# Local attention's values: two projected spans of 128 tokens a batch instead of three

## Chip, cores and metric

The kernel runs on one core of one Trainium2 chip. The metric is the device time of one execution in microseconds, taken as the median of several runs. All data are float32 except a few bfloat16 copies of weights outside the part that changes.

## What is computed

A two-layer decoder block on `x` (4 batches of 256 tokens, width 256) with a context of 1601 tokens a batch: sliding-window attention, attention over the context, a quantised feed-forward part, a second attention, a linear attention over the context and a mixture of experts, each followed by a residual and a layer norm. The change is in the first part, the sliding-window attention with 16 heads of 16. Cut to what matters:

```python
C = 64                                              # chunk and window
kc = concatenate([kp[:, :, :-1], kp[:, :, 1:]], -2) # keys: the chunk before, and this chunk
vc = concatenate([vp[:, :, :-1], vp[:, :, 1:]], -2)
diff = C + qa[:, None] - ka[None, :]
mask = (diff >= 0) & (diff <= WINDOW)               # and the key's position not negative
scores = where(mask, einsum('bhncd,bhnkd->bhnck', qc, kc) * SCALE, -inf)
out = einsum('bhnck,bhnkd->bhncd', softmax(scores), vc)
```

A query attends to itself and to the 64 tokens before it. The values are `x @ w_v`, one row for each token; softmax and the weighted sum don't depend on the order in which a query's keys stand, as long as scores, mask and values have the same order.

## The kernel before

The whole program is one function, `decoder`. Its helper functions don't issue instructions as they are called: they record operations, and `Loom.weave` (line 309) then plays the program through as a list scheduler. It takes each time the operation that can start earliest by assumed durations (`Side.cost`, line 402, and the figure given to each `piece` of TensorE work), with an order of priorities to break ties, and lets idle engines of one part work on another part. The order on every engine, of the DMA issues too, is thus written out when the program is built; on the chip, each engine runs its own list in order and waits on semaphores. Because one helper issues everything, all lines of the profile on DVE, ACT and POOL read L398, all matmuls L261, all transposes L268 and all ordinary loads L275; a group is told by its tiles.

`l0_attention(b)` (line 673) is recorded for the four batches with the highest priority. After the queries and keys of a batch (`qT`, `kT`, the latter in two copies for the even and odd heads of a pair, each with the other's rows at zero) come the values. Tile `v` (two of them, for even and odd batches) has the shape (128 tokens, 3 spans, 8 head pairs, 2, 32); the half of the last axis that isn't written stays at the zero that POOL put there at the start. Before, three spans of 128 tokens are projected, starting at token 0, 64 and 128 (span `i` starts at 64 x i): two matmuls of 128x256 each (the width of 256 is summed in two halves), and then one copy on DVE for the even heads and one on ACT for the odd ones.

`unit(j)` (line 696) does eight heads. Its first piece, "scores", has four matmuls for queries 0 to 127 against keys 0 to 127 (tiles of 32 rows by 128 columns of the array, one for each pair of heads), and then eight for the other queries: 64 queries 128 to 191 against keys 64 to 191 (`c` = 0), and 64 queries 192 to 255 against keys 128 to 255 (`c` = 1), in tiles of 32 rows by 64 columns. Each of the four score banks then gets the mask `wmask` added on DVE, a softmax (maximum on DVE, four exponentials on ACT, a reciprocal on DVE, a product on DVE or POOL), four transposes into a bank, and an evacuation into `aT`. The last piece, "pv", multiplies with span 0 for the queries 0 to 127, span 1 for 128 to 191 and span 2 for 192 to 255. Two such units make a batch; an output projection, residual and norm follow.

Around it, with a lower priority, `context_sums` (line 764) works on the context for the linear attention of the second layer: pieces "keys" (`KT` by `wkv1`), a feature map on ACT and DVE (`fm`, `kf`), pieces "sums" (`V` by `kf`), and an addition on POOL (`kacc`). Those sums, and products of weights for later layers, fill TensorE while local attention's softmax runs, and continue after it. All score, projection and transpose results go through one pool of eight PSUM banks (`bank`).

The masks are made at the start on POOL: a memset of `wmask` (128 x 2 x 128) and of a helper tile `lower`, two selections (`keep_where`, line 555) for each of three masks, and a copy on DVE of the lower half of the second mask out of `lower`.

Of the kernel before, what the change touches and what calls it, by code (L numbers as in the profile page):

```python
# [31 lines left out]
P = 128  # L32
# [10 lines left out]
NEG = -1e30  # L43
# [138 lines left out]
class Loom:  # L182
# [62 lines left out]
    @contextmanager  # L245
    def piece(self, us, claims=(), ins=(), over=(), what=""):


        self.cur = ([], [], list(ins))
        yield  # L250
        fns, outs, ins = self.cur
        self.cur = None
        read = [o for v in over for _, o in v.buf.reads]
        self.op({"PE": (us, us, lambda: [f() for f in fns])}, outs, ins, claims, after=read, what=what)

    def mm(self, o, lhsT, rhs, start, stop, **kw):
        fns, outs, ins = self.cur
        outs.append(o)
        ins += [v for v in (lhsT, rhs) if isinstance(v, View)]
        fns.append(  # L260
            lambda: self.nc.tensor.matmul(real(o), real(lhsT), real(rhs), start=real(start), stop=stop, **kw)  # L261
        )

    def turn(self, o, x, ident):
        fns, outs, ins = self.cur
        outs.append(o)
        ins += [x, ident]
        fns.append(lambda: self.nc.tensor.transpose(real(o), real(x), real(ident)))  # L268
# [156 lines left out]
def decoder(ctx: ExitStack, tc: tile.TileContext, a: dict, out: bass.AP):  # L425
    nc = tc.nc
    k = Loom(tc)
# [39 lines left out]
    def bank(shape=(P, 512), dtype=F32, acc=False):  # L467
        return psB.tile(shape, dtype, "bank", free=True, acc=acc)
# [20 lines left out]
    def evac(dst, src):  # L489

        return either((k.vector, "tensor_copy", (dst, src), {}), (k.scalar, "copy", (dst, src), {}))
# [63 lines left out]
    def keep_where(t, pattern, base, cm, fill):  # L555
        k.gpsimd.affine_select(
            out=t, in_=t, pattern=pattern, compare_op=ALU.is_ge, fill=fill, base=base, channel_multiplier=cm
        )
# [3 lines left out]

    wmask = p1w.tile((P, 2, P), F32, "wmask")
    lower = p1.tile((P, 2, 2, P), F32, "at", bufs=7)[:, 0, 0]
    k.gpsimd.memset(wmask, 0.0)
    k.gpsimd.memset(lower, 0.0)
    for m, off in ((wmask[:, 0], 0), (wmask[:, 1], 64), (lower, 0)):
        keep_where(m, [[-1, P]], off, 1, NEG)
        keep_where(m, [[1, P]], 64 - off, -1, NEG)
    k.vector.tensor_copy(wmask[64:, 1], lower[64:])  # L570

    hmask = const.tile((P, 8, 17), F32, "hmask")
# [15 lines left out]
    for i in range(2):  # L588
        v = p1w.tile((P, 3, H // 2, 2, 32), F32, f"v{i}")
# [10 lines left out]
    def new_x():  # L600
        return xpool.tile((P, 2, D), F32, "x")
# [29 lines left out]
    def norm(b, x):  # L631
        X[b], XT[b] = x, new_xt()
        norm_into(x, XT[b])

    def softmax(at):

        n = at.shape[2]
        nm, ss, rs = (tiny((P, 4), tag) for tag in ("nm", "ss", "rs"))
        k.vector.tensor_reduce(nm, at, AX.X, ALU.max, negate=True)
        for i in range(4):  # L640
            k.scalar.activation(at[:, i], at[:, i], AF.Exp, bias=nm[:, i : i + 1], accum_out=ss[:, i : i + 1])
        k.vector.reciprocal(rs, ss)
        args = (at, at, rs.unsqueeze(2).to_broadcast([P, 4, n]), ALU.mult)
        either((k.gpsimd, "tensor_tensor", args, {}), (k.vector, "tensor_tensor", args, {}))
# [18 lines left out]
    def project_in(xt, w, claims=(), what=""):  # L663

        ps = bank((P, 2, S))
        with piece(1.73, claims, what=what):
            for j in range(2):
                for c in range(2):
                    mm(ps[:, j, :], w(c, j), xt[:, c, :], c == 0, c == 1)
        return ps  # L670


    def l0_attention(b):
        pool = p1


        kT = pool.tile((P, 2, 2, S), F32, "kT")
        ps = project_in(XT[b], lambda c, j: wqkv[:, c, D + j * P : D + (j + 1) * P], [kT], "k")
        k.vector.tensor_scalar(kT[:, :, 0, :], ps, qmask[:, 0:1], None, ALU.mult)
        k.scalar.activation(kT[:, :, 1, :], ps, AF.Copy, scale=qmask[:, 1:2])  # L680
        qT = pool.tile((P, 2, S), F32, "qT")
        ps = project_in(XT[b], lambda c, j: wqkv[:, c, j * P : (j + 1) * P], [qT], "q")
        evac(qT, ps)
        v = vs[b % 2]
        for i in range(3):
            pv = bank((P, D))
            with piece(0.86, over=[v], what="v"):
                for c in range(2):
                    mm(pv, XT[b][:, c, 64 * i : 64 * i + P], wqkv[:, c, 2 * D :], c == 0, c == 1)
            heads = pv.rearrange("p (h u e) -> p h u e", u=2, e=16)  # L690
            k.vector.tensor_copy(v[:, i, :, 0, :16], heads[:, :, 0, :])
            k.scalar.copy(v[:, i, :, 1, 16:], heads[:, :, 1, :])
        xn = new_x()
        oT = pool.tile((P, 2, S), F32, "oT1", bufs=1)

        def unit(j):

            quarters = [slice(32 * r, 32 * r + 32) for r in range(4)]
            pss = [bank((P, 2, 2, P)) for _ in range(4)]
            ats = [pool.tile((P, 2, 2, P), F32, "at", bufs=7) for _ in range(4)]  # L700
            with piece(1.5, ats, what="scores"):
                for rr, ps in zip(quarters, pss):
                    mm(ps[:, 0], qT[rr, j, :P], kT[rr, j, :, :P], True, True, skip_group_check=True)
                for c in range(2):
                    for r, (rr, ps) in enumerate(zip(quarters, pss)):
                        mm(
                            ps[64 * c : 64 * c + 64, 1],
                            qT[rr, j, P + 64 * c : P + 64 * c + 64],
                            kT[rr, j, :, 64 + 64 * c : P + 64 + 64 * c],
                            True, True, skip_group_check=True,  # L710
                            tile_position=(32 * r, 64 * c),
                        )
            aTs = []
            for ps, at in zip(pss, ats):
                k.vector.tensor_tensor(at, ps, wmask.unsqueeze(2).to_broadcast([P, 2, 2, P]), ALU.add)
                at = at.rearrange("p t u k -> p (t u) k")
                softmax(at)
                pt = bank((P, 4, P))
                aT = pool.tile((P, 2, 2, P), F32, "aT", bufs=4)
                with piece(0.44, [aT], what="turn"):  # L720
                    for i in range(4):
                        turn(pt[:, i], at[:, i], ident)
                evac(aT.rearrange("p t u q -> p (t u) q"), pt)
                aTs.append(aT)
            po = bank((P, S))
            with piece(1.5, [oT], what="pv"):
                for i, q0, n in ((0, 0, P), (1, P, 64), (2, P + 64, 64)):
                    t = q0 // P
                    for u in range(2):
                        for r, rr in enumerate(quarters):  # L730
                            mm(
                                po[rr, q0 : q0 + n],
                                v[:, i, 4 * j + r, u, :],
                                aTs[r][:, t, u, q0 - t * P : q0 - t * P + n],
                                u == 0, u == 1, skip_group_check=True,
                                tile_position=(0, 32 * r),
                            )
            evac(oT[:, j], po)

        for j in range(2):  # L740
            unit(j)
        for t in range(2):
            py = bank((P, D))
            with piece(0.86, [xn], what="out"):
                for j in range(2):
                    mm(py, oT[:, j, t * P : (t + 1) * P], w0o[:, j, :], j == 0, j == 1)
            k.vector.tensor_tensor(xn[:, t, :], py, X[b][:, t, :], ALU.add)
        norm(b, xn)
# [719 lines left out]
    for b in range(B):  # L1468
        at_prio(0, b)
        l0_attention(b)  # L1470
# [47 lines left out]
    for b in range(B):  # L1518
        at_prio(7, b)
        for ts, x, xt in l1_attention(b):  # L1520
# [5 lines left out]
            if b == B - 1:  # L1526
                at_prio(8)
                n = EARLY[ts[0]]
# [93 lines left out]
```

## Time and profile before

| | |
|---|---|
| median of 3 runs | 708.22 us (708.21 to 709.07) |
| the profiled execution's own time | 710.24 us |
| its span | 708.5 us |
| TensorE busy | 664.6 us |
| VectorE (DVE) busy | 447.3 us |
| ScalarE (ACT) busy | 297.4 us |
| GpSimd (POOL) busy | 126.4 us |
| DMA | 87.33 MB, mean 123 GB/s |
| granted TensorE clock, mean | 0.982 |

The profile is of one execution. PE stands for matmuls and PEld for the loading of the stationary operand. A float32 matmul shows as two records of matmul and two of weight loading, which are its two passes; a transpose shows as one. Matmul records overlap, so that the distance between their starts tells more than their lengths. Counts (x...) are of records. A line of groups ends with the idle time of the engine just before the instructions and what ended it.

### The profile page before, as it was taken

How to read it: one execution, taken by the hardware profiler on the slowest of the kernel's cores; microseconds unless marked ns; L12 is line 12 of the kernel's file. 1: busy time of each engine (PE TensorE's matmuls, PEld its weight loads, DVE VectorE, ACT ScalarE, POOL GpSimd, SP SyncE). 2: the span in 40 equal slices, each digit the busy share in tenths (PEclk: the TensorE clock that was granted, in tenths of full speed). 3: DMA queues.
4: the chain of work that ended last, by engine and by line, in shares of the span. 5: the costliest groups of instructions: out<-in, count | busy, mean ns of one | idle time of the engine just before them, and what ended most of it. 6: DMA issues, size and time to landing. Idle time of an engine off the chain costs nothing.

```text
span 708.5 us, 12388 instructions
## 1 busy us (share of the span) xinstructions
PE 664.6 (94%) x4407; PEld 531.2 (75%) x4411; DVE 447.3 (63%) x1155; ACT 297.4 (42%) x930; POOL 126.4 (18%) x170
## 2 busy tenths in 40 slices
PE   7999999999999999999899999999998899999970
PEld 5787878568877777767676777767766898999960
DVE  4878896333528634384799978687686555333336
ACT  2868965211132433343358777476455121111100
POOL 3313223012300000000022011221213213111112
PEclk9999999999999999999999999999999999999995
DMA  8922100646998241000010600000002845976405
GB/s 302 351 76 76 52 19 10 205 128 224 331 300 283 67 149 37 1 1 1 0 54 1 237 3 1 1 31 1 30 1 73 318 147 195 364 278 228 147 26 177
DMA packets 62673, 87.33 MB, mean 123 GB/s; under 512 B 4654, under 2 KB 44340, under 8 KB 62612
## 3 DMA queue, kind: packets, MB, share of 16 engines
q1 hardware_dynamic: 60740, 81.40, 35.2%
q0 software_dynamic: 1872, 5.13, 2.0%
q8 instruction: 36, 0.59, 0.3%
q14 instruction: 25, 0.20, 0.1%
HBM read 70.83 MB, written 15.69 MB: 122 GB/s over the span
## 4 chain that ended last, share of the span: by engine, by line
PE 78%; DVE 14%; ACT 3%; DMA 2%; issue 1%; POOL 1%; SPq 0%; POOLq 0%; DVEq 0%
PE bank L261 70%; PE bank L268 8%; DVE at L398 3%; ACT at L398 3%; DVE nm L398 2%; DVE x L398 1%; DVE h L398 1%; POOL rstd L398 1%; DVE as L398 1%; DVE entry L398 1%; DVE st L398 1%; DMA wt<-in_w 1%; DMA back<-yd 1%; DVE kf L398 0%; DVE fm L398 0%
## 5 line engine op out<-in xcount | busy, mean ns | idle before, releaser
L398 ACT ACTIVATE at<-at,nm 128x128 f32<-128x128 f32 (+1 forms) x256 | 106.5, 420 | 25.7 <-DVE nm L398 25.2
L261 PE MATMUL bank<-xgT,wt 128*128 128x128 f32 x736 | 87.0, 278 | 0.8 <-DVE xgT L398 0.5
L261 PEld LDWEIGHTS bank<-xgT,wt 128*128 128x128 f32 x736 | 86.2, 195 | 2.0 <-DVE xgT L398 0.8
L268 PE MATMUL bank<-ident,at 128*128 128x128 f32 (+1 forms) x440 | 61.5, 277 | 1.8 <-DVE at L398 1.6
L268 PEld LDWEIGHTS bank<-ident,at 128*128 128x128 f32 (+1 forms) x440 | 50.8, 142 | 14.3 <-issue 5.9
L261 PE MATMUL bank<-V,aT 128*128 128x256 f32 (+1 forms) x240 | 55.2, 380 | 0.7 <-DVE o L398 0.6
L261 PE MATMUL bank<-KT,qT 128*128 128x512 f32 (+1 forms) x128 | 54.0, 553 | 0.0
L261 PEld LDWEIGHTS bank<-V,aT 128*128 128x128 f32 (+1 forms) x240 | 45.2, 190 | 11.2 <-issue 3.6
L398 POOL TENSOR_SCALAR rstd<-mv 128x2 f32<-128x2 f32 (+1 forms) x26 | 6.5, 251 | 261.6 <-DVE mv L398 215.8
L261 PE MATMUL bank<-kf,V 128*128 128x256 f32 (+1 forms) x208 | 50.4, 383 | 1.1 <-DVE kf L398 1.1
L398 DVE TENSOR_REDUCE nm<-at 128x4 f32<-128x512 f32 (+1 forms) x64 | 50.6, 807 | 0.4
L261 PE MATMUL bank<-wkv,KT 128*128 128x256 f32 (+1 forms) x208 | 49.7, 382 | 0.0
L398 ACT ACTIVATION_READ_ACCUMULATOR at<-at,nm 128x1 f32 x256 | 48.7, 190 | 0.0
L398 ACT ACTIVATE eh<-bank 128x512 f32<-128x512 f32 x23 | 13.7, 597 | 77.5 <-PE bank L261 77.5
L261 PEld LDWEIGHTS bank<-kf,V 128*128 128x128 f32 (+1 forms) x208 | 38.2, 190 | 7.5 <-DVE kf L398 2.3
L398 ACT COPY aT<-bank 128x512 f32<-128x512 f32 (+2 forms) x60 | 31.5, 551 | 29.4 <-PE bank L268 28.6
L261 PE MATMUL bank<-w2e,eh 128*128 x184 | 43.4, 380 | 0.0
L261 PEld LDWEIGHTS bank<-wkv,KT 128*128 128x128 f32 (+1 forms) x208 | 37.8, 186 | 7.3 <-issue 1.5
L398 DVE TENSOR_TENSOR at<-at,rs 128x512 f32<-128x512 f32 (+1 forms) x43 | 39.7, 924 | 0.8
L398 POOL TENSOR_TENSOR at<-at,rs 128x512 f32<-128x512 f32 (+1 forms) x21 | 23.6, 1123 | 87.9 <-DVE rs L398 74.7
L398 ACT ACTIVATE fm<-bank 128x512 f32<-128x512 f32 (+2 forms) x33 | 18.1, 552 | 46.6 <-PE bank L261 46.6
L1258 POOL DMA_INDIRECT yd<-ey,slots x23 | 22.3, 971 | 83.9 <-DVE slots L398 81.9
(246 smaller groups left out, 1231.3 us busy)
## 6 DMA issues: line engine op xcount, KB each, us to landing
wt<-in_w SPq DMA_DIRECT2D x46, 512.0 KB, 4.7
lists<-h SPq DMA_DIRECT2D x6, 1548.0 KB, 16.8
KT<-in_ctxT SPq DMA_DIRECT2D x6, 1024.0 KB, 5.1
V<-in_ctx SPq DMA_DIRECT2D x6, 1024.0 KB, 5.4
w2e<-in_w SPq DMA_DIRECT2D x8, 512.0 KB, 9.1
KT<-in_ctxT SPq DMA_DIRECT2D x6, 577.0 KB, 3.8
V<-in_ctx SPq DMA_DIRECT2D x6, 512.0 KB, 4.0
xg<-lists SPq DMA_DIRECT2D x23, 129.0 KB, 4.3
```

The source lines that it names most:

```text
L261: lambda: self.nc.tensor.matmul(real(o), real(lhsT), real(rhs), start=real(start), stop=stop, **kw)
L268: fns.append(lambda: self.nc.tensor.transpose(real(o), real(x), real(ident)))
L398: return getattr(engine, method)(*[real(x) for x in args], **{k: real(x) for k, x in kw.items()})
L1258: d = nc.gpsimd.indirect_dma_start(out=dst.real(), out_offset=bass.IndirectOffsetOnAxis(ap=row.real(), axis=0), in_=src.real(), in_offset= ...
```

## The change

Only two spans of values are projected in each batch, tokens 0 to 127 and 128 to 255 (`i` = 0 and 2). Span 1 of `v`, which serves the queries 128 to 191 and so needs the tokens 64 to 191, is copied out of the same two banks: partitions 64 to 127 of the first (tokens 64 to 127) stay on partitions 64 to 127, and partitions 0 to 63 of the second (tokens 128 to 191) stay on 0 to 63. Its keys thus stand in another order, 128 to 191 first and 64 to 127 second. The scores for these queries are made in that order: one matmul of 2x128 columns for each pair of heads becomes two of 2x64, with the same stationary operand. Their mask (partitions 0 to 63 of `wmask[:, 1]`) is made anew: forbidden where the key's column is greater than the query's row and less than the row + 64. Each batch has four copies into `v` on DVE and four on ACT, two of each over 128 partitions and two over 64.

```diff
-    k.gpsimd.memset(wmask, 0.0)
+    k.gpsimd.memset(wmask[:, 0], 0.0)
     k.gpsimd.memset(lower, 0.0)
-    for m, off in ((wmask[:, 0], 0), (wmask[:, 1], 64), (lower, 0)):
+    for m, off in ((wmask[:, 0], 0), (lower, 0)):
         keep_where(m, [[-1, P]], off, 1, NEG)
         keep_where(m, [[1, P]], 64 - off, -1, NEG)
+    k.gpsimd.memset(wmask[:64, 1], NEG)
+    keep_where(wmask[:64, 1], [[1, P]], -1, -1, 0.0)
+    keep_where(wmask[:64, 1], [[-1, P]], 63, 1, 0.0)
     k.vector.tensor_copy(wmask[64:, 1], lower[64:])
...
-        for i in range(3):
+
+        for i in (0, 2):
             pv = bank((P, D))
             with piece(0.86, over=[v], what="v"):
                 for c in range(2):
                     mm(pv, XT[b][:, c, 64 * i : 64 * i + P], wqkv[:, c, 2 * D :], c == 0, c == 1)
             heads = pv.rearrange("p (h u e) -> p h u e", u=2, e=16)
-            k.vector.tensor_copy(v[:, i, :, 0, :16], heads[:, :, 0, :])
-            k.scalar.copy(v[:, i, :, 1, 16:], heads[:, :, 1, :])
+            part = slice(0, 64) if i else slice(64, P)
+            for rr, n in ((slice(0, P), i), (part, 1)):
+                k.vector.tensor_copy(v[rr, n, :, 0, :16], heads[rr, :, 0, :])
+                k.scalar.copy(v[rr, n, :, 1, 16:], heads[rr, :, 1, :])
...
-                for c in range(2):
+                for c, to, k0, n in ((0, 0, P, 64), (0, 64, 64, 64), (1, 0, P, P)):
                     for r, (rr, ps) in enumerate(zip(quarters, pss)):
                         mm(
-                            ps[64 * c : 64 * c + 64, 1],
+                            ps[64 * c : 64 * c + 64, 1, :, to : to + n],
                             qT[rr, j, P + 64 * c : P + 64 * c + 64],
-                            kT[rr, j, :, 64 + 64 * c : P + 64 + 64 * c],
+                            kT[rr, j, :, k0 : k0 + n],
                             True, True, skip_group_check=True,
                             tile_position=(32 * r, 64 * c),
                         )
```

## The prediction, made before the changed kernel ran

> **What bounds the kernel now.** I read the page first (busy shares, then the shares of the chain), then busy time by stage, then the chain of waits in order of time inside the stage that the change touches, then the tiles `v`, `wqkv` and `kT`. Page, parts 1 and 4:
>
> ```profile
> span 708.5 us, 12388 instructions
> PE 664.6 (94%) x4407; PEld 531.2 (75%) x4411; DVE 447.3 (63%) x1155; ACT 297.4 (42%) x930; POOL 126.4 (18%) x170
> PE 78%; DVE 14%; ACT 3%; DMA 2%; issue 1%; POOL 1%; SPq 0%; POOLq 0%; DVEq 0%
> ```
>
> TensorE is the bound over all. Whether it is so where the change lies is asked of the stages. Local attention (`l0_attention`) runs from 4 to about 123 us, woven with context sums, which go on with weight products to 197 us; the first scores of cross attention start at 200 us. Busy times by stage:
>
> ```profile
> 4.00:30.00 26.00, 24.52 (x183) 19.36 (x184) 17.11 (x33) 13.56 (x46) 7.64 (x8) 1.00 1.04 364
> 30.00:66.00 36.00, 36.00 (x315) 29.83 (x313) 29.91 (x67) 27.98 (x119) 8.64 (x9) 1.00 0.33 101
> 66.00:111.00 45.00, 44.00 (x481) 35.10 (x478) 42.07 (x95) 36.20 (x152) 10.96 (x12) 1.00 0.14 40
> 111.00:124.00 13.00, 13.00 (x109) 11.03 (x108) 7.65 (x17) 4.64 (x12) 4.94 (x6) 1.00 0.05 14
> ```
>
> The columns are PE, PEld, DVE, ACT, POOL, clock, DMA share and GB/s. From 30 to 66 us PE is never idle and DVE has a sixth free. From 66 to 111 us DVE is busy 42.07 of 45 us, and PE idles 1.0. The chain of waits says the same:
>
> ```profile
> 58.23 6.40 PE bank L261 x72
> 64.63 0.87 PE bank L268 x8
> 65.50 1.38 PE bank L261 x24
> 66.89 0.00 issue
> 66.89 0.68 DVE kf L398
> ...
> 109.73 0.70 DVE at L398
> 110.43 0.04 issue
> 110.48 0.66 PE bank L268 x4
> 111.14 1.73 PE bank L261 x8
> ```
>
> Up to 66.9 us the chain is PE work, then 43.6 us of DVE and ACT steps alone (masks, maxima, exponentials, copies), then PE again. A PE saving ahead of 66.9 us should reach the end; one inside that stretch can be lost as idle PE time, unless context work is moved into it.
>
> **What the skill says.** "Perfetto Trace Analysis", Identifying the Most-Contended Engine, warns that matmul busy time is no measure of PE's limit, since matmuls are pipelined. The trace agrees: one 128x256 record lasts 379 ns, but twelve in a row take 2.75 us, and the next group begins 2.68 us after the first began. So I price matmuls by the distance of starts (0.216 us) and not by duration. "TensorEngine Tiling (Array Packing)", Key Properties, says that tiles work independently and that a change of tiling mode drains the array. The trace agrees with both: eight score matmuls of 32x64 tiles, two records each, take 0.62 us together, and the last full record before the first score takes 0.31 instead of 0.216 us. "TensorE: Matmul & The Clock Gate", The mechanism (Part 3), says that matmuls keep strict program order. Here the trace doesn't quite agree: the second record of a tile's matmul starts 0.267 us after its first, while the other seven tiles' first records start in between, within 0.05 us. I use that rule only for an upper price below.
>
> **What goes away.** Each batch loses one of three value projections: two matmuls, shown as four records. Tiles `wqkv`, `v` and `kT`:
>
> ```profile
> L261 PE MATMUL bank<-wqkv,xt x48: 379/379/483, 10.8 to 77.9; 128*128 128x256 f32 x48
> L398 DVE COPY v<-bank x12: 252/276/292, 11.9 to 82.3; 128x128 f32<-128x128 f32 x12
> L398 ACT COPY v<-bank x12: 239/262/267, 12.2 to 78.3; 128x128 f32<-128x128 f32 x12
> L261 PE MATMUL bank<-kT,qT x192: 374/400/478, 13.5 to 100.8; 32*64 32x256 f32 x128, 32*128 32x256 f32 x64
> ```
>
> 48 records become 32: 16 x 0.216 = 3.46 us of PE time, 0.864 a batch. The projections of batches 0, 1 and 2 start at 10.8, 31.2 and 45.0 us, all before 66.9; those of batch 3 at 70.5 and 77.2, inside the DVE stretch. So 2.59 us of the 3.46 are on the path for sure, and 0.86 only if the weave fills the hole.
>
> **What is added on PE.** For queries 128 to 191 the score matmul of 2x128 keys becomes two of 2x64 with the same stationary operand: 4 more matmuls (8 records) in each of 8 units, columns unchanged. Now, the round lasts 0.62 us: weights 0.053, two passes of 0.213, a drain. The split tile needs 0.053 + 4 x 0.107 = 0.48 us, as long as the unsplit neighbour beside it, weights being loaded under the running pass. If the neighbour (queries 192 to 255, issued last) still starts at once, the price is nothing: tiling covers it. If it starts only when the split tile's second matmul has started, 0.21 us later, the price is 8 x 0.21 = 1.7 us. If it waits for the whole of it, 8 x 0.43 = 3.4 us. The trace of before has no tile with two matmuls queued behind each other and another tile behind them in a 32x64 mode, so these are the bounds; a gain I exclude, since no column goes away. I take 0.85 us, half way between the first two.
>
> **What is added on DVE and ACT.** Each batch has 4 copies into `v` on each, not 3. Two of the four take 64 partitions; by the by-form groups a 65-partition step is no cheaper for that (ACT `fm` 65x256: 362 ns, ACT `oT` copy 128x256: 362). So 4 x 0.275 = 1.1 us DVE and 4 x 0.257 = 1.0 us ACT. Batch 0's fall where DVE had waited 0.57 us for PE between copies: nothing. Those of batches 1 and 2 stand where PE is the bound and DVE has 6 of 36 us free: nothing, as long as that cover lasts. Batch 3's stand on the DVE chain: 0.28, plus up to 0.26 if ACT's is on it too. I take 0.3. Behind these copies on DVE wait the masks and maxima that ACT's exponentials wait for, and on ACT the exponentials that DVE's reciprocals wait for. A projection's bank is freed after four copies instead of two, but two banks are taken instead of three.
>
> **What moves.** The masks on POOL: two memsets (about 0.2 us each, by the 128x128 one's 205 ns) replace one of 0.31, the six selections stay six, all before 4 us; the first mask is used at 14.9 us: nothing, covered by the first load and projections. No DMA is added or removed, and SP's and POOL's queues are passed by no step. But the order on all engines is planned in `weave` from assumed durations, so an 0.86 piece less and two copies more in each batch may order neighbours anew. Known stalls that such a change can remove or repeat:
>
> ```profile
> 14.74 5.45 PE L261 MATMUL bank<-wkv,KT 128*128 128x256 f32 x24
> 21.32 1.99 PE L261 MATMUL bank<-kf,V 128*128 128x256 f32 x8 [1.13 <-DVE kf L398]
> ```
>
> That one is 1.13 us, those of 66 to 111 us sum to 1.0. After 200 us the stages contain far more idle time between small steps (PE idle 8 of 80 us from 480 to 560), so 2 us either way is fair for an order that differs. Nothing there is tied to an absolute time: beyond the first load, PE waits for no DMA before 200 us, and SP's loads wait for PE to free buffers; they come earlier with it.
>
> **The sum.** -2.59 (batches 0 to 2) - 0.43 (half of batch 3's) + 0.85 (scores) + 0.3 (copies) = -1.9 us. The profiled execution had a span of 708.5 and a time of 710.24, so about 1.7 us lie around the span, and it is 2.0 us above the median of the runs, 708.22; the difference is applied to the median: 706.3 us. Its own range, from full filling and free scores (-3.46 + 0.3) to dear scores with batch 3's hole lost (-2.59 + 1.7 + 0.5), is 705.1 to 707.8.
>
> **Rivals.**
> - *The score rounds eat it.* Strict order of matmuls makes the neighbour wait for both halves: 3.4 us against 3.46 saved. About 708.2, no change. For it: in-order issue; against it: eight tiles overlap now.
> - *DVE and ACT become the bound of all of local attention (slower).* Place: 30 to 111 us. DVE is at 93% from 66 us on; if the PE time removed turns into waits on it, the whole saving is lost and three batches' added copies are in series on the chain, 3 x (0.275 + 0.257) = 1.6 us: 709.8. It decides once PE's idle time from 30 to 111 us grows from 1.0 us by the whole saving there, 2.6. Against it: context sums and weight products, 197 - 123 = 74 us more of them, are there to fill PE.
> - *The new order matters more than the work*: some stalls vanish (the 1.13 above, a part of those later), and the time is 2 us under the sum: 704.3; or as much above it.
>
> **Chances.** The sum 0.50, score rounds 0.15, DVE/ACT bound 0.13, a luckier order 0.16, an unlucky one 0.06. What a measurement of this kernel can tell from no change is about 0.2%, 1.4 us: faster is below 706.8. Of the sum's case two thirds and a little more lie there, with the luckier order and parts of the rest: faster 0.60, same 0.23, slower 0.17. Range 703.4 to 709.8: it takes in the luckier order's middle, the no-change rival and the edge of the slower one.
>
> **What would show it.** Right: `wqkv,xt` 32 records, 16 copies of `v` on DVE and 16 on ACT (12 now), PE's idle time up to 200 us as before, the first scores of cross attention (`KT,qT`, 199.95 us) earlier by about 2. `kT,qT` has 256 records; the second score round 0.62 us (free), 0.83 (one round late) or 1.05 (serial) answers the score term. Wrong: PE idle in 66 to 111 us grown to 2 us or more says that DVE holds the stage; a start of cross attention earlier by 2 to 3 us with an end that is not says that the later order gave it back.

## The result, and the profile after

The changed kernel takes 706.36 us (median of 11 runs, 704.97 to 707.82), the kernel before beside it 709.45 (11 runs, 708.21 to 710.1): a ratio of 0.9959, 95% interval 0.9950 to 0.9968, by which the change is 2.9 us faster. (The 708.22 us of the table before is the median of the first three of these 11 runs.) The profiled execution took 706.43 us with a span of 704.7. The page of the changed kernel, parts 1 and 4:

```profile
span 704.7 us, 12480 instructions
PE 659.4 (94%) x4455; PEld 528.6 (75%) x4459; DVE 448.9 (64%) x1161; ACT 297.5 (42%) x933; POOL 125.4 (18%) x170
PE 79%; DVE 13%; ACT 4%; DMA 1%; issue 1%; POOL 1%; SPq 0%; POOLq 0%; DVEq 0%; ACTq 0%
```

PE runs 48 more instructions in 5.2 us less busy time; DVE is busy 1.6 us longer. The tiles `v`, `wqkv` and `kT` of the changed kernel:

```profile
L398 DVE COPY v<-bank x16: 260/288/295, 12.0 to 76.1; 128x128 f32<-128x128 f32 x8, 64x128 f32<-64x128 f32 x8
L398 ACT COPY v<-bank x16: 246/260/266, 12.3 to 75.8; 128x128 f32<-128x128 f32 x8, 64x128 f32<-64x128 f32 x8
L261 PE MATMUL bank<-wqkv,xt x32: 379/379/483, 10.9 to 74.6; 128*128 128x256 f32 x32
L261 PE MATMUL bank<-kT,qT x256: 267/346/478, 12.7 to 104.3; 32*64 32x128 f32 x64, 32*128 32x256 f32 x32, 32*64 32x256 f32 x32
```

Counts are as forecast. Busy time by stage (columns as before), for the two stages in question:

```profile
30.00:66.00 36.00, 35.52 (x348) 28.85 (x347) 34.45 (x76) 30.11 (x129) 10.33 (x10) 1.00 0.28 89
66.00:111.00 45.00, 43.88 (x490) 35.38 (x489) 38.66 (x89) 32.80 (x137) 8.45 (x10) 1.00 0.21 64
```

DVE's full stretch has moved: it is now from 30 to 66 us (34.45 of 36, before 29.91), and from 66 to 111 us DVE has more room (38.66 of 45, before 42.07). The chain of waits shows the same: it leaves PE at 37.1 us and comes back at 77.35, 40.2 us on DVE and ACT instead of 43.6. Batch 3's copies into `v` stand on it:

```profile
36.29 0.76 PE bank L268 x5
37.05 0.06 issue
37.11 0.68 DVE aT L398
...
75.45 0.21 DVE v L398
75.66 0.02 issue
75.69 0.43 ACT v L398 x2
76.11 0.02 issue
76.14 0.28 DVE v L398
76.42 0.89 DVE x L398
77.31 0.04 issue
77.35 0.76 PE bank L268 x4
78.12 7.21 PE bank L261 x76
```

So the list scheduler didn't only drop a piece: it wove local attention's softmax and the context sums in another order. TensorE's timeline shows where it stands idle now (brackets: idle before, and what ended it):

```profile
20.55 1.99 PE L261 MATMUL bank<-kf,V 128*128 128x256 f32 x8 [1.12 <-DVE kf L398]
...
52.25 0.63 PE L268 MATMUL bank<-ident,at 128*128 128x128 f32 x4 [0.40 <-DVE at L398]
...
77.35 0.76 PE L268 MATMUL bank<-ident,x 128*128 128x128 f32 x4 [1.08 <-DVE x L398]
```

The first stall is the old one, unchanged (1.13 us before). The other two are new; the last comes 2.4 us after batch 3's second value projection has ended (73.95 to 74.98 us). Of the prediction's signs, PE's idle time from 66 to 111 us stayed at 1.1 us, under the 2 us that would have said that DVE holds that stage. From the first matmul to 200 us it wasn't quite "as before": 2.7 us, before 2.1.

How far the two kernels are apart is best read at landmarks on TensorE, of one profiled execution each:

| start of, us | before | after | difference |
|---|---|---|---|
| first matmul | 4.36 | 5.39 | +1.03 |
| first value projection | 10.80 | 10.87 | +0.07 |
| first scores of local attention | 13.48 | 12.69 | -0.79 |
| first scores of cross attention | 199.95 | 197.10 | -2.85 |
| end of the span | 708.54 | 704.72 | -3.82 |

The first row is the arrival of a weight, which differs in each execution; the second shows that it costs nothing here, because fewer matmuls then run at the slow pace of the start (427 ns from start to start; 14 such steps before, 9 after). From the first value projection to cross attention the gain is 2.93 us (differences are taken before rounding): 0.86 in the first batch, 2.07 in the stretch from the first scores of local attention to those of cross attention (186.47 us before, 184.40 after; "the stretch" below). The last row's further 1.0 us isn't read as an effect: from the first scores of cross attention to the end the profiles of all kernels below take 507.6 to 510.7 us, in no order with what was changed. From 205 us on, both traces show the same order of groups on TensorE, DVE, ACT and POOL.

### The profile page after: what moved, and what is told of

The parts are those of the page before. It is cut to its first block, busy times and chain, and to the rows that moved or that the text cites. A ratio compares the mean times of both kernels' runs of the same rounds, so it can differ in the third digit from the quotient of the medians.

```text
span 704.7 us, 12480 instructions
## 1 busy us (share of the span) xinstructions
PE 659.4 (94%) x4455; PEld 528.6 (75%) x4459; DVE 448.9 (64%) x1161; ACT 297.5 (42%) x933; POOL 125.4 (18%) x170
## 2 busy tenths in 40 slices
DMA packets 62673, 87.33 MB, mean 124 GB/s; under 512 B 4654, under 2 KB 44340, under 8 KB 62612
## 4 chain that ended last, share of the span: by engine, by line
PE 79%; DVE 13%; ACT 4%; DMA 1%; issue 1%; POOL 1%; SPq 0%; POOLq 0%; DVEq 0%; ACTq 0%
PE bank L261 70%; PE bank L268 9%; ACT at L398 3%; DVE at L398 3%; DVE nm L398 2%; DVE x L398 1%; DVE h L398 1%; POOL rstd L398 1%; DVE as L398 1%; DVE entry L398 1%; DVE st L398 1%; DMA wqkv<-in_wqkvT 1%; DMA back<-yd 1%; DVE fm L398 0%; DVE hq L398 0%
## 5 line engine op out<-in xcount | busy, mean ns | idle before, releaser
L261 PE MATMUL bank<-xgT,wt 128*128 128x128 f32 x736 | 85.3, 275 | 0.5 <-DVE xgT L398 0.5
L261 PEld LDWEIGHTS bank<-xgT,wt 128*128 128x128 f32 x736 | 84.5, 192 | 1.5 <-DVE xgT L398 0.8
L398 DVE TENSOR_REDUCE m<-bank 128x1 f32<-128x512 f32 (+1 forms) x32 | 20.5, 640 | 26.3 <-PE bank L261 26.1
```

What stands on the lines that cost most here:

```text
L398: return getattr(engine, method)(*[real(x) for x in args], **{k: real(x) for k, x in kw.items()})
```

## The experiments

The kernel before took 711 to 712 us beside them; device times are therefore compared as ratios, and the finer reading is the stretch. It comes from one profiled execution of each kernel. Where two kernels have the same order, that is enough: the first four runs below show, on TensorE, DVE, ACT and POOL, the order of groups of the kernel that they start from, and from 124 to 197 us, where they change nothing, TensorE's starts keep their distance to that kernel's within 0.001 us.

**The split scores alone.** In the kernel before, the old key order kept:

```diff
-                for c in range(2):
+                for c, to, k0, n in ((0, 0, 64, 64), (0, 64, P, 64), (1, 0, P, P)):
...
-                            ps[64 * c : 64 * c + 64, 1],
+                            ps[64 * c : 64 * c + 64, 1, :, to : to + n],
...
-                            kT[rr, j, :, 64 + 64 * c : P + 64 + 64 * c],
+                            kT[rr, j, :, k0 : k0 + n],
```

> The kernel before with one part of the change alone: the score matmul of queries 128 to 191 split into two of 2x64 columns, keys in their old order, three projections and three copies as before; the order of all engines is that of before. Theory (tiles run side by side, the unsplit neighbour starts at once): the second score round goes from 0.62 to 0.64 us, +0.2 us over 8 units, 709.7 us against 709.45, the first scores of cross attention at 200.2 us instead of 199.95. Rival (the neighbour waits for the split tile's second matmul): round 0.83 us, +1.7 us, 711.1 us. Rival (serial): 1.05 us, +3.4 us, 712.9 us.

Ratio 1.0008 (0.9992 to 1.0024), stretch 186.60, cross attention at 200.15. TensorE's weight loads in the kernel before, and in this one:

```profile
14.12 0.23 PEld L261 LDWEIGHTS bank<-kT,qT 32*64 32x64 f32 x16 [0.33 <-issue]
14.74 0.30 PEld L261 LDWEIGHTS bank<-wkv,KT 128*128 128x128 f32 x2 [0.39 <-issue]
```

```profile
14.19 0.42 PEld L261 LDWEIGHTS bank<-kT,qT 32*64 32x64 f32 x24 [0.33 <-issue]
14.83 0.51 PEld L261 LDWEIGHTS bank<-wkv,KT 128*128 128x128 f32 x3 [0.22 <-issue]
```

The round from the first load of 32x64 tiles to the next full-array load lasts 0.64 us; before, it was 0.62. In the changed kernel it is 0.64 us too (13.33 to 13.98 us). The neighbour starts at once, and the split is nearly free: 0.13 us over eight units.

**TensorE's work put back**, in the order of the changed kernel:

```diff
-                for c in range(2):
+                for c in [0, 1] * (i // 2 + 1):
```

> The changed kernel with the removed TensorE work put back: the projection of the second span is issued twice into the same bank, 48 records of value projection as before the change, planned at the old length, so that the order of all engines is that of the changed kernel. Theory (TensorE time is what was saved): +3.46 us on the changed kernel's 706.4, about 709.8, first scores of cross attention at 200.5 us instead of 197.1. Rival (the gain is a luckier order of the engines' lists): stays near 706.4. Rival (DVE and ACT hold local attention, PE time there is slack): +1 us or less, 707.4.

Ratio 0.9986 (0.9975 to 0.9997), so 0.27% or 1.9 us slower than the changed kernel's 0.9959 (0.9 to 2.9 us, an estimate from the two intervals), not 3.46. The profile tells why. Set side by side with the changed kernel, instruction by instruction, TensorE falls behind by 0.86 us at the extra projection of each batch. Of batch 1's, 0.20 us are made up at waits soon after, and 0.32 of batch 2's; batch 3's costs nothing at all:

```profile
75.33 1.89 PE L261 MATMUL bank<-wqkv,xt 128*128 128x256 f32 x8
77.15 1.36 PE L261 MATMUL bank<-kT,qT 32*128 32x256 f32 x32
78.73 0.76 PE L268 MATMUL bank<-ident,x 128*128 128x128 f32 x4 [0.22 <-DVE x L398]
```

Its longer projection (8 records, not 4) only shortens the wait for DVE's `x` from 1.08 to 0.22 us. From the first value projection (10.10 us here, by an earlier end of the slow pace) to cross attention (198.47) this kernel takes 2.15 us more than the changed one: of the 3.46 us removed, 2.15 reached cross attention. It is also 0.78 us quicker over this way than the kernel before, although it does all of that kernel's projections, and the split scores and added copies on top: so much, at least, is the new order's.

**A short third projection in the order of before:**

```diff
-                    mm(pv, XT[b][:, c, 64 * i : 64 * i + P], wqkv[:, c, 2 * D :], c == 0, c == 1)
+                    x, w = XT[b][:, c, 64 * i : 64 * i + P], wqkv[:, c, 2 * D :]
+                    if i == 1:
+                        x, w = (t.bitcast(BF16).rearrange("p (n u) -> p n u", u=2)[:, :, 1] for t in (x, w))
+                    mm(pv, x, w, c == 0, c == 1)
```

> The kernel before, with the middle one of the three value projections made from the upper halves of the float32 words as bfloat16: one pass instead of two with weight loading as before, everything else and the order of all engines as before. By half a pass per record pair, 2 x 0.107 us instead of 0.864 us a batch, 2.6 us of TensorE time go away in the old order. Theory (TensorE's time reaches the end wherever it is taken away): 709.45 - 2.6 = 706.8 us. Theory of the prediction (batch 3's part, 0.65, is lost in the stretch that DVE and ACT hold): 707.5. Rival (the gain was the new order): 709.4.

Ratio 1.0001 (0.9987 to 1.0015); cross attention at 199.03, 0.93 us earlier. Of that, 0.14 us come before the first value projection and 0.64 between it and the first scores; the stretch is 186.32 against 186.47, only 0.15 less. TensorE gains 0.64 us at each of the four short projections. It keeps batch 0's, and of the other three it gives back 0.43, 0.50 and 0.72 us at the waits that follow, of which these show:

```profile
37.62 0.63 PE L268 MATMUL bank<-ident,at 128*128 128x128 f32 x4 [0.24 <-ACT kT L398]
...
50.77 0.63 PE L268 MATMUL bank<-ident,at 128*128 128x128 f32 x4 [0.30 <-DVE at L398]
```

```profile
74.47 1.32 PE L261 MATMUL bank<-kT,qT 32*128 32x256 f32 x20 [0.20 <-ACT v L398]
```

In the kernel before, the same groups (of eight and 24 records, in one piece) show no wait:

```profile
38.16 1.04 PE L268 MATMUL bank<-ident,at 128*128 128x128 f32 x8
...
51.45 1.04 PE L268 MATMUL bank<-ident,at 128*128 128x128 f32 x8
...
75.00 1.80 PE L261 MATMUL bank<-kT,qT 32*128 32x256 f32 x24
```

In the old order, then, DVE and ACT held local attention from batch 1 on, already between 30 and 66 us, where TensorE showed no idle time at all. The expectation of 707.5 us, which had only batch 3's part lost, fell, and so did that of 706.8; by device time the rival's "no change" held, though batch 0's 0.64 us did come through to cross attention.

**Without the copies into span 1**, order of the changed kernel:

```diff
-                k.vector.tensor_copy(v[rr, n, :, 0, :16], heads[rr, :, 0, :])
-                k.scalar.copy(v[rr, n, :, 1, 16:], heads[rr, :, 1, :])
+                for side, method, dst, src in (
...
+                    k.op({side.name: (busy, us, emit if n != 1 else lambda: None)}, [dst], [src], what=method)
```

> The changed kernel without the copies into span 1 of the values (planned, but not issued: 2 of 4 copies a batch on DVE and on ACT are left out, so that the values of queries 128 to 191 stay zero), order otherwise the same. Theory (copies are covered by TensorE work): within 0.3 us of the changed kernel, 706.1 to 706.4, though DVE is busy 16 x 0.14 to 0.28 = 2.2 us less. Rival (they stand on the chain of DVE and ACT in local attention): 1 to 3 us faster, 703.4 to 705.4.

Ratio 0.9946 (0.9928 to 0.9964; against the changed kernel's 0.9959 the intervals overlap), stretch 183.57, 0.83 us less. The wait ahead of `ident,x` is 0.72 us instead of 1.08:

```profile
76.53 0.76 PE L268 MATMUL bank<-ident,x 128*128 128x128 f32 x4 [0.72 <-DVE x L398]
```

Against the changed kernel, TensorE is 0.25 us ahead by 69 us, before batch 3's copies (71.2 to 76.4 us), and 0.83 after them. The copies aren't covered: they cost 0.8 us, 0.58 of it at batch 3's and 0.25 at those of batches 1 and 2. (In the changed kernel a 64-partition copy is no cheaper than one of 128: 286 ns mean on DVE against 284.)

**The same work in other orders.** The changed kernel and the kernel before, each with other assumed lengths of pieces in the plan and nothing else changed:

```diff
-            with piece(0.86, over=[v], what="v"):
+            with piece(1.29, over=[v], what="v"):
```

> The changed kernel with its two value pieces planned at 1.29 us instead of 0.86 (so that the plan gives them together what the three had before), which orders the engines' lists anew; the work is that of the changed kernel. Read from the first scores of local attention to the first scores of cross attention: 186.47 us before the change, 184.41 us after. Theory (the order is worth 1 to 2 us by itself: the work of before with the changed kernel's order took 185.69 with dearer copies and scores): anywhere from 183.5 to 186. Rival (work alone counts): 184.2 to 184.6.

> The kernel before, its three value pieces planned at 0.573 us each (together what the changed kernel's two get), work unchanged. Same stretch, 186.47 us before. Theory (order is worth 1 to 2 us): 184.5 to 186. Rival (work alone counts): 186.3 to 186.7.

> The changed kernel with values planned at 0.90 instead of 0.86 us a piece, work unchanged: one more draw of the order. Theory (order): 184 to 187 us in the stretch, not the same as 184.40. Rival (work alone): 184.2 to 184.6.

> The kernel before with values planned at 0.90 us a piece, work unchanged. Theory (order): 185 to 187.5 us in the stretch, and the mean over the four plans of each work (0.86, the equal total, 0.90, measured) 0.5 to 1.5 us shorter after the change. Rival (work alone): 186.3 to 186.7, and 2 us shorter after the change in every plan.

```diff
-            with piece(1.5, ats, what="scores"):
+            with piece(1.3, ats, what="scores"):
...
-            with piece(1.5, [oT], what="pv"):
+            with piece(1.02, [oT], what="pv"):
```

> The changed kernel, planned with the lengths that the trace shows for scores (1.3 instead of 1.5 us) and products with values (1.02 instead of 1.5); work unchanged. Stretch from the first scores of local attention to the first of cross attention: 184.40 us in the changed kernel, 186.77 in its other order with values planned at 1.29. Theory (the order is worth 1 to 2 us, and a truer plan leaves fewer waits): 183.5 to 184.5, device time 706 or less on the chip of the first runs. Rival (a plan's truth doesn't matter, each order is a draw): 184.5 to 187. Rival (work alone): 184.2 to 184.6.

> The kernel before, with the same truer plan; work unchanged. Stretch 186.47 us before. Theory (the order decides, and the work's own part in this stretch is 1 us or less): within 1 us of the changed kernel under the same plan, on either side. Rival (work alone): 2 us longer than the changed kernel under the same plan.

| values planned at | stretch, before's work | stretch, changed work |
|---|---|---|
| 0.86 (the two kernels) | 186.47 | 184.40 |
| 0.573 (before), 1.29 (changed) | 186.53 | 186.77 |
| 0.90 | 187.64 | 186.53 |
| 0.86, scores and products as measured | 185.66 | 183.16 |
| mean | 186.58 | 185.22 |

Each number is one execution of one order. The rival "work alone" falls: the same work takes 183.2 to 186.8 us. The theory's ranges didn't all hold either. The changed kernel came out above both ranges at 1.29 and inside the theory's at 0.90; the kernel before came out in the rival's range at 0.573 and just above the theory's at 0.90. Under the truer plan the two works lie 2.50 us apart, as "work alone" said of this pair, and not within 1 us. The rows differ by 2.07, -0.24, 1.11 and 2.50 us, so the mean difference of 1.36 us lies in the expected 0.5 to 1.5, but with a standard error of about 0.6 us, an estimate from these four.

With the values planned at 1.29 the changed kernel loses the whole gain of the stretch; its two stages:

```profile
30.00:66.00 36.00, 34.73 (x318) 28.51 (x317) 31.75 (x70) 28.01 (x118) 9.83 (x10) 1.00 0.35 111
66.00:111.00 45.00, 43.53 (x505) 34.71 (x504) 39.95 (x89) 32.51 (x132) 12.11 (x13) 1.00 0.11 32
```

TensorE idles 1.27 + 1.47 us there, the changed kernel 0.48 + 1.12. Two of its waits make up most of it:

```profile
50.81 0.63 PE L268 MATMUL bank<-ident,at 128*128 128x128 f32 x4 [0.98 <-DVE at L398]
78.16 0.76 PE L268 MATMUL bank<-ident,x 128*128 128x128 f32 x4 [1.12 <-DVE x L398]
```

The truer plan gave the shortest stretch of either work, and for the changed kernel a ratio of 0.9941 (0.9923 to 0.9960), the lowest of all; it can't be told from the changed kernel's 0.9959. Four orders of each work aren't enough to say that a truer plan is better as a rule.

**Span 1 copied elsewhere.** On POOL, or by DMA:

```diff
-            for rr, n in ((slice(0, P), i), (part, 1)):
-                k.vector.tensor_copy(v[rr, n, :, 0, :16], heads[rr, :, 0, :])
-                k.scalar.copy(v[rr, n, :, 1, 16:], heads[rr, :, 1, :])
+            k.vector.tensor_copy(v[:, i, :, 0, :16], heads[:, :, 0, :])
+            k.scalar.copy(v[:, i, :, 1, 16:], heads[:, :, 1, :])
+            k.gpsimd.tensor_copy(v[part, 1], v[part, i])   # or: k.dma_start(v[part, 1], v[part, i])
```

> The changed kernel with span 1 of the values copied on POOL out of spans 0 and 2 (two copies of 64x512 a batch, zeros with them) instead of two half copies each on DVE and ACT out of the banks. Theory (the span-1 copies cost 0.75 us on the DVE and ACT chain of local attention, POOL is idle): stretch 183.7 us, 0.7 us less than the changed kernel's 706.4 us. Rival (POOL's copies hold DVE back, or come late for the products with values): no gain or slower, stretch 184.4 or more.

> As the one with POOL, but span 1 is copied by two DMAs a batch issued on SP, 128 KB each. Theory: nothing on the compute engines, values are needed 10 us later, stretch 183.7 us. Rival (SP's list is in order, the copies stand behind loads that wait for TensorE to free a buffer): products with values wait for them, stretch over 186 us, slower than before the change.

POOL: ratio 0.9991 (0.9980 to 1.0002), stretch 187.77. DMA: 0.9969 (0.9950 to 0.9988), stretch 184.96. These two stretches can't be set beside the others: both orders have only one of batch 0's two projections ahead of the first scores (0.96 us from the first projection to the scores, in the changed kernel 1.82), so that 0.86 us more lie in the stretch. From the first value projection to cross attention POOL takes 188.73 us and DMA 185.92, the changed kernel 186.22 and the kernel before 189.16. So POOL loses most of the gain, while DMA is 0.3 us ahead by the trace and by its ratio can't be told from the changed kernel. The expected gain of 0.7 us isn't seen in either, and DMA's rival, over 186 us, fell. Both are orders of their own, so that they don't price the copies; the run without copies in the changed order does. The DMAs landed 2.2 to 5.7 us after their issue, and TensorE's `aT,v` products, planned later (the first at 43.9 us instead of 27.7), show no wait for them.

## Why the prediction came out right

The time forecast was 706.3 us, the measured 706.36, though against a median of 709.45 for the kernel before in the same comparison: forecast -1.9 us, measured -2.9. Both lie in the range, but that the two times agree to 0.1 us is luck: the median that the forecast started from, of three runs, was 1.2 us lower than that of 11, and the gain was 1.0 us larger. The terms are less well met than their sum: with the order as it was drawn, the work gave less than forecast, and the order made up for more than that.

- *Removed TensorE work of batches 0 to 2, -2.59 forecast.* In the changed order it is worth 0.86 + 0.66 + 0.54 = 2.1 us (put-back run). In the old order little more than batch 0's reached cross attention (0.64 us of it, and 0.15 of the three others' 1.9 together). The step that failed is "A PE saving ahead of 66.9 us should reach the end". In the kernel before, TensorE had no idle time from 30 to 66 us, and still gave most of batches 1 and 2's saving back at the next waits, where it now stood until DVE and ACT were done (0.24 us for `kT`, 0.30 for `at`).
- *Batch 3's part, -0.43 forecast (half of 0.86).* None: it became part of the wait of 1.08 us at 77.35, which is 0.22 with the work put back.
- *Scores, +0.85 forecast.* +0.13 measured. The half-way value was mis-sized; the lower bound, that tiles run side by side, was right, and the upper prices, for which a neighbour waits its turn in program order, never applied.
- *Copies, +0.3 forecast.* +0.83. Most of it, 0.58, is batch 3's, about the 0.28 + 0.26 that the prediction gave for copies of both engines on the chain but didn't take whole. The other 0.25 are batches 1 and 2's, put at nothing because DVE was only 83% busy there. In the new order it is busy 34.45 of those 36 us, which is the likely reason.
- *Masks, DMA, queues: nothing.* POOL's selections on the mask still end before 4 us, DMA's bytes are the same, 87.33 MB.
- *Order: none forecast, 2 us either way in the range.* With these terms the work comes to -2.1 + 0.1 + 0.8 = -1.2 us; measured from the first value projection it was -2.93. The remaining 1.7 us are the new order, by subtraction. That assumes that the terms add up, though the scores were priced in the old order, and the copies with the projections already gone; what is shown without this assumption is 0.8 us (the put-back run against the kernel before). Over four plans each, the work gave -1.36 us in the stretch and -0.86 in the first batch, -2.2 us, which agrees with the forecast sum within its standard error of about 0.6 us; the order actually drawn for the changed kernel was the second best of its four by the stretch.

Of the rivals, the score rounds fell by the first run. The DVE and ACT bound was half right: in the old order it took nearly all of what was saved after batch 0, but it didn't in the new one, where PE's idle time from 30 to 111 us grew from 1.0 to 1.6 us and not by the 2.6 that this rival asked for. The luckier order, given 0.16, is in the result beside the sum: it turned 1.2 us of work into 2.9, by the same subtraction.

What stays open: which placement in the new order brings its gain, and how far above the 0.8 us shown that gain lies; the 1.7 us rest on adding terms up. The runs don't show its place.

## What to carry to other kernels

Where a scheduler writes the order of all engines, a small edit is two changes, its work and a new draw of the order; price the first by runs that keep the order (work put back at the same planned length, or cut at the same planned length), and see the second by changing a planned length alone. No idle time on an engine over a stage doesn't make it the bound of that stage: look at how narrowly the other engines' results arrive. Splitting a matmul in one tile of the array while an equally long one ran in the next cost almost nothing here (0.13 us in eight rounds). And a stretch between two landmarks can be compared only when the same work lies between them.

## What was not expected of the hardware

In the split score round the neighbouring tile's matmul, issued after both halves, started 0.05 us into the round, before the second half of the split one (0.27 us): each tile kept the order of its own matmuls, but the tiles together didn't keep the program's. The slow pace at the start wasn't a fixed amount: in the 14 profiles, 8 to 15 steps of mostly 427 ns, 3.5 to 6.4 us in all, came before the first of 216. In the changed kernel the first weight arrived 1.03 us later than before, and the first value projection started only 0.07 us later.
